# Additions of the diagonal behind all selects of their step, sums multiplied later, next block's rows loaded a phase sooner

## The chip, the cores and the metric

The kernel runs on one core of a Trainium2 chip. The metric is the device time of one execution in microseconds. Five engines matter: PE (TensorE, the matrix products), ACT (ScalarE, exponentials and copies), DVE (VectorE, row maxima and small vector work), POOL (GpSimd, masking and additions in SBUF) and SP (SyncE, which issues all transfers). Each engine runs its own instructions in program order and waits on semaphores for the others.

## What is computed

A pre-norm transformer layer in float32 on two sequences of 2048 rows and 512 columns: causal attention with 16 heads of 32 and rotary positions, then a linear layer to which two of eight low-rank experts are added per row.

```python
x = x + _L0_attn_ref(_layernorm(x), Wq, Wk, Wv, Wo)
x = x + _L0_ffn_ref(_layernorm(x), base_w, base_b, router_w, router_b, lora_A, lora_B)
# attention:
scores = jnp.einsum('bhqd,bhkd->bhqk', q, k) / math.sqrt(dk)
scores = jnp.where(causal[None, None], scores, -jnp.inf)
attn = jax.nn.softmax(scores, axis=-1)
ctx = jnp.einsum('bhqk,bhkd->bhqd', attn, v)
```

## The kernel before, in words

**Blocks and steps.** The 4096 rows are eight blocks of 512 (`BLK`), four per sequence; block `n` has place `j = n % 4` in its sequence. The 16 heads are four groups `g` of four. A step is one pair (block, group), written (n,g) here: 32 steps. In a step the keys up to the block's end are `NT*(j+1)` tiles of 128, of which the last four lie on the diagonal. A tile of the step with number `kt` is worked on for four heads at once.

**Two streams side by side.** `side_by_side` interleaves, on every engine, the row maxima of the next step (`row_maxima`, tiles `sm`, L384 to L405) with the weighing of the current one (`attend`). For each tile, `attend` multiplies keys with queries (`scores`, L523), subtracts the maxima with a second product (`shift`, L531), lets ACT take the exponentials into a tile `pt` (`weigh`, L546) and, on a diagonal tile, lets POOL zero what lies above the diagonal (the select, `affine_select`, L553). A tile of 512 columns is handled as two pairs of heads, so each diagonal tile has two selects. Tiles 1 and 3 of the diagonal share one buffer and one select, so that a step has three diagonal quads with six selects: the first tile, the pair, and the third tile.

**Phases.** Each `yield` of `side_by_side` ends a phase. Between phases the main loop hands out everything else: products due now (`between`), projections and the former block's output stages from the list `waiting` (paced by `credit`), entries of `aside` (loads, layer norms, parts of the division) and additions from `ready`. A tile whose `weigh` is over is multiplied with the values three phases later (`later(3, ...)`, `weighted`, L595, tile `av`). PE is in order, so a product that waits holds everything behind it.

**Sums of the weights.** The softmax denominators need the sum over all `pt` tiles. POOL adds tiles into the step's first tile, which has a buffer of its own kind (tag `acc`, two buffers): `add`, L616, one instruction per pair of heads. For the middle tiles of long steps (`SUMMED`) ACT sums beside the row maxima instead. So a step has adds for the diagonal tiles, and in blocks with j = 2 and 3 also for tiles 1 to 3. Each add is put on `ready` where its exponentials are issued. Every gap between phases drains `ready` from the front while the head's step is `weighed`, that is, while the step's first tile has been multiplied with the values. Before a tile takes one of the three `pt` buffers, `before` forces the adds and products of that buffer's former tile. After the last product of a step, ACT copies `av` away and `later(2, ...)` sets `summed`: it drains what is left of the step's adds and multiplies the sum tile with ones on PE (L623, tile `den`). The sums then go through DRAM to be spread over partitions (L649, L652), are inverted on DVE (`over_sums`, three phases later), come back broadcast (L658), and POOL multiplies the context by them (`over_all`, L665, three phases later again).

**Next block.** `start_block` sets four row loads (`xa`, L104, on SP, with the rotation tables behind the fourth), their layer norm (moments on DVE and POOL, scaling on ACT) and their transposition (`turned`, L159 on PE, L160 on ACT) at phases counted back from the block's begin by `EARLY` = 14; the first key projection (`kps`, L193) follows the last transposition. The row tiles share five buffers (tag `tmp`) with the rotation products, the normalised rows of the output stages and the tile `total` of the sums.

The cross-engine order on PE, ACT, DVE and POOL is the order in which these functions issue; the order on SP is chosen by the framework. The lines that the change touches: L560 (what is put on `ready`), `after` (L573), L611 (`later`), L766 to L769 (the phases of the next block) and L856 (the draining).

Of the kernel before, what the change touches and what calls it, by code (L numbers as in the profile page):

```python
# [23 lines left out]
NB = S // BLK  # L24
# [10 lines left out]
def preln_attention_moe_lora(  # L35
# [428 lines left out]
    ready = []  # L464

    def later(phases, tile, do):
        due.append((phase[0] + phases, tile, do))
        due.sort(key=lambda entry: entry[0])
# [19 lines left out]
    def attend(s):  # L488

        n, g, q, keys, values = s["n"], s["g"], s["q"], s["k"], s["v"]  # L490
        j = blocks[n][1]
        diagonal, beside = NT * j, SUMMED[j]

        summed_from = 0 if beside[0] else NT * beside[1]
        tiles = NT * (j + 1)
# [3 lines left out]
        pts, index = {}, {}  # L499
        s["av"] = None  # L500

        def low(kt):
            return max(kt - diagonal, 0) * P
# [7 lines left out]
        def quad(*kts):  # L511

            all_of = slice(0 if len(kts) > 1 else low(kts[0]), BLK)
            sc = {}

            def take(r):
                sc[r] = bank(f"sc_{n}_{g}_{kts[0]}_{r}")

            def scores(i, r):
                if i < len(kts):  # L520
                    jj, tt = divmod(kts[i], NT)
                    rows = slice(DK * r, DK * r + DK)
                    nc.tensor.matmul(  # L523
                        out=sc[r][:, place(kts[i])], lhsT=keys[jj][rows, bass.ts(tt, P)],
                        rhs=q[rows, low(kts[i]) :], start=True, stop=False,
                    )

            def shift(i, r):
                if i < len(kts):
                    rows = slice(DK * r, DK * r + 3)  # L530
                    nc.tensor.matmul(  # L531
                        out=sc[r][:, place(kts[i])], lhsT=ones_b[rows, :],
                        rhs=s["max"][rows, low(kts[i]) :], start=False, stop=True,
                    )

            def weigh(r):
                if kts[0] not in pts:
                    tag, bufs = ("acc", 2) if kts[0] == summed_from else ("pt", PTS)
                    pt = p2.tile(
                        [P, 4, BLK], F32, tag=tag, bufs=bufs, name=f"pt_{n}_{g}_{kts[0]}"  # L540
                    )
                    begun[0] += tag == "pt"
                    for kt in kts:
                        index[kt], pts[kt] = begun[0] if tag == "pt" else 1 << 30, pt
                pt = pts[kts[0]]
                nc.scalar.activation(pt[:, r, all_of], sc[r][:, all_of], AF.Exp)  # L546
                if kts[0] >= diagonal and r % 2:

                    at = all_of.start
                    on = pt[:, r - 1 : r + 1, at : at + len(kts) * P]  # L550
                    if len(kts) > 1:
                        on = on.rearrange("p h (k q) -> p h k q", q=P)
                    nc.gpsimd.affine_select(  # L553
                        out=on, in_=on, compare_op=ALU.is_ge, fill=0.0, base=0,
                        pattern=[[0, 2]] + [[0, len(kts)]] * (len(kts) > 1) + [[1, P]],
                        channel_multiplier=-1,
                    )
                if kts[0] != summed_from and not beside[0] <= kts[0] // NT < beside[1] and r % 2:
                    ready.extend(
                        (index[kts[0]], s, summed_from, lambda kt=kt: add(kt, r - 1)) for kt in kts  # L560
                    )

            def before():

                if kts[0] == summed_from:
                    return
                last = begun[0] + 1 - PTS
                while any(tile <= last for _, tile, _ in due):
                    due.pop(0)[2](2)
                while ready and ready[0][0] <= last:  # L570
                    ready.pop(0)[3]()

            def after():  # L573
                if len(kts) == 1:
                    lo = low(kts[0])
                    mid = (lo + BLK) // 2
                    halves = [(kts[0], lo, mid), (kts[0], mid, BLK)]
                else:
                    halves = [(kt, low(kt), BLK) for kt in kts]
                later(3, index[kts[0]], lambda many: weighted(halves, many))  # L580

            return before, take, scores, shift, weigh, after

        def weighted(halves, many):

            if s["av"] is None:
                s["av"] = ps_o.tile([P, BLK], F32, tag="av", name=f"av_{n}_{g}")
            whole = len(halves) == many == 2 and halves[0][0] == halves[1][0]
            now, left = halves[:many], halves[many:]
            for kt, lo, hi in [(halves[0][0], low(halves[0][0]), BLK)] if whole else now:  # L590
                jj, tt = divmod(kt, NT)
                at = place(kt).start - low(kt)
                for r in range(4):
                    rows = slice(DK * r, DK * r + DK)
                    nc.tensor.matmul(  # L595
                        out=s["av"][rows, lo:hi],
                        lhsT=values[jj][g][:, tt, rows],
                        rhs=pts[kt][:, r, at + lo : at + hi],
                        start=(kt == 0 and lo == 0),
                        stop=(kt == tiles - 2 and hi == BLK),  # L600
                    )
            if left:
                due.insert(0, (0, index[left[0][0]], lambda many: weighted(left, many)))
                return
            kt = halves[-1][0]
            if kt == summed_from:
                s["weighed"] = True
            if kt == tiles - 2:
                s["dest"] = wide.tile([P, BLK], F32, tag="ctx", bufs=6, name=f"ctx_{n}_{g}")
                nc.scalar.copy(s["dest"], s["av"])  # L610
                later(2, 1 << 31, summed)  # L611

        def add(kt, r):

            some = pts[summed_from][:, r : r + 2, low(kt) :]
            nc.gpsimd.tensor_add(some, some, pts[kt][:, r : r + 2, place(kt)])  # L616
# [134 lines left out]
    def set_aside(at, do):  # L751
        aside.append((at, do))
        aside.sort(key=lambda entry: entry[0])

    def wait(stage, at, not_before=0):
        waiting.append((at, len(waiting), not_before, stage))
        waiting.sort(key=lambda entry: entry[:2])

    def start_block(n):

        (load, measured, scaled, turned), heads, vals, made = prepare(n)
        keys[n], values[n], queries[n], contexts[n] = made["k"], made["v"], made["q"], []
        at = begin[NC * n]
        for t in range(NT):
            if n > 0:
                set_aside(at - EARLY + t, lambda t=t: load(t))  # L766
                set_aside(at - EARLY + 2 + t, lambda t=t: measured(t))
                set_aside(at - EARLY + 4 + t, lambda t=t: scaled(t))
                wait([(0.5, lambda t=t: turned(t))], at - 7 + t, at - 8 + t)  # L769
            else:  # L770
                load(t)
        if n == 0:
            for do in (measured, scaled, turned):
                for t in range(NT):
                    do(t)
        for g in range(NC):
            for i, stage in enumerate(heads[g]):
                if n == g == 0:
                    do_stage(stage)
                else:  # L780
                    here = begin[NC * n + g]

                    free = begin[NC * n + g - 1] + 3 if i else 0
                    wait(stage, here - 4 + i, max(free, at - 6))
            if g == 1:
                for stage in vals:
                    wait(stage, begin[NC * n + 1] + 1, at - 6)
# [9 lines left out]
    EARLY, BEHIND, AHEAD = 14, 3, 100  # L797
# [4 lines left out]
    for step in steps + [None]:  # L802
        maxima = []
        if step:
            n, g = step
# [4 lines left out]
            while len(queries[n]) <= g:  # L810
                do_stage(waiting.pop(0)[3])
            first = n - blocks[n][1]
            s = {
                "n": n, "g": g, "q": queries[n][g], "ctx": contexts[n],
                "k": [keys[m][g] for m in range(first, n + 1)],
                "v": [values[m] for m in range(first, n + 1)],
            }
# [3 lines left out]
        for i in range(slots):  # L821
# [3 lines left out]
            for _ in side_by_side(*todo):  # L825
# [27 lines left out]
                    given = given or us > 0.0  # L853
                if not given:
                    ahead()
                while ready and ready[0][1].get("weighed"):  # L856
                    ready.pop(0)[3]()
        late = part(weights, slots - 1, slots)
        if step:
            split()  # L860
            before, turned = s, turned_next
# [60 lines left out]
```

## Time and profile before

| | before |
|---|---|
| median of 3 runs | 2009.55 us (2005.08 to 2010.38) |
| the profiled execution's own time | 2002.71 us |
| its span, first to last instruction | 2000.9 us |
| mean granted TensorE clock | 0.966 |
| ACT busy | 1100.6 us |
| DVE busy | 1030.6 us |
| POOL busy | 936.8 us, of which L616 540.4 us and L553 92.7 us |
| DMA queues | 9.5% of 16 engines' span |
| chain that ended last | PE 77%, POOL 10%, ACT 6%, DVE 4% |

A group row of the profile reads: line, engine, operation, output<-inputs, shape, count | busy us, mean ns of one | idle us of that engine just before these instructions, and what ended most of it. "PEclk" in the slices is the clock that the throttle granted to TensorE, in tenths of full speed. POOL's groups on the critical lines:

```profile
L616 POOL TENSOR_TENSOR pt<-pt,pt 128x768 f32<-128x768 f32 (+2 forms) x320 | 540.4, 1702 | 65.2 <-PE av L595 35.2
L553 POOL TENSOR_SCALAR_AFFINE_SELECT pt<-pt 128x256 f32<-128x256 f32 (+1 forms) x192 | 92.7, 485 | 319.1 <-ACT pt L546 319.1
```

The chain by line, in the same execution, has 20% on L523, 11% on L595, 7% on L384 and 6% on POOL's L616.

### The profile page before, as it was taken

How to read it: one execution, taken by the hardware profiler on the slowest of the kernel's cores; microseconds unless marked ns; L12 is line 12 of the kernel's file. 1: busy time of each engine (PE TensorE's matmuls, PEld its weight loads, DVE VectorE, ACT ScalarE, POOL GpSimd, SP SyncE). 2: the span in 40 equal slices, each digit the busy share in tenths (PEclk: the TensorE clock that was granted, in tenths of full speed). 3: DMA queues.
4: the chain of work that ended last, by engine and by line, in shares of the span. 5: the costliest groups of instructions: out<-in, count | busy, mean ns of one | idle time of the engine just before them, and what ended most of it. 6: DMA issues, size and time to landing. Idle time of an engine off the chain costs nothing.

```text
span 2000.9 us, 34243 instructions
## 1 busy us (share of the span) xinstructions
PE 1869.0 (93%) x12880; PEld 760.7 (38%) x12880; DVE 1030.6 (52%) x2856; ACT 1100.6 (55%) x2653; POOL 936.8 (47%) x906
## 2 busy tenths in 40 slices
PE   7889989999989999998989999999999999999988
PEld 3334433334333333333334434333433333433434
DVE  3545555456555556563155556456555555555503
ACT  1346653456546676684533546545647466656851
POOL 3563434257464536154476344236545645434462
PEclk9899989899999999998999999999999999998999
DMA  4000111001200000100000112100011000020001
GB/s 163 22 12 13 55 32 43 6 7 39 78 14 7 1 28 28 59 23 1 22 18 18 38 59 70 51 15 7 22 49 59 2 6 7 22 65 7 7 7 43
DMA packets 42271, 61.19 MB, mean 31 GB/s; under 512 B 13180, under 2 KB 13692, under 8 KB 42104
## 3 DMA queue, kind: packets, MB, share of 16 engines
q1 hardware_dynamic: 42104, 59.00, 9.5%
q8 instruction: 101, 1.65, 0.3%
q14 instruction: 66, 0.54, 0.1%
HBM read 50.08 MB, written 8.90 MB: 29 GB/s over the span
## 4 chain that ended last, share of the span: by engine, by line
PE 77%; POOL 10%; ACT 6%; DVE 4%; issue 3%; DMA 1%; SPq 0%; ACTq 0%; POOLq 0%; DVEq 0%
PE sc L523 20%; PE av L595 11%; PE sm L384 7%; POOL pt L616 6%; PE qps L193 6%; PE kps L193 6%; PE vps L218 6%; PE yps L332 6%; PE ops L249 6%; PE sc L531 3%; ACT sm L405 3%; ACT pt L546 2%; PE den L623 1%; POOL pt L553 1%; PE yps L339 1%
## 5 line engine op out<-in xcount | busy, mean ns | idle before, releaser
L546 ACT ACTIVATE pt<-sc 128x512 f32<-128x512 f32 (+1 forms) x1152 | 600.2, 584 | 654.3 <-PE sc L531 570.3
L384 PE MATMUL sm<-k,q 32*128 32x512 f32 (+3 forms) x2560 | 691.6, 587 | 10.9 <-DVE pm L426 5.5
L397 DVE TENSOR_REDUCE pm<-sm 128x1 f32<-128x512 f32 x768 | 491.4, 684 | 318.1 <-PE sm L384 280.3
L523 PE MATMUL sc<-q,k 32*128 32x512 f32 (+3 forms) x2560 | 628.6, 588 | 2.6 <-ACT pt L546 1.5
L616 POOL TENSOR_TENSOR pt<-pt,pt 128x768 f32<-128x768 f32 (+2 forms) x320 | 540.4, 1702 | 65.2 <-PE av L595 35.2
L595 PE MATMUL av<-pt,v 128*32 128x256 f32 (+3 forms) x3440 | 330.2, 462 | 79.7 <-POOL pt L553 72.0
L405 ACT ACTIVATE sm<-sm,pm 128x512 f32<-128x512 f32 x512 | 345.2, 687 | 18.6 <-DVE pm L397 18.0
L392 DVE CUSTOM_DVE_ANT_0 sm<-sm,mask 128x128 f32<-128x128 f32 (+3 forms) x512 | 244.9, 512 | 130.0 <-PE sm L384 84.2
L523 PEld LDWEIGHTS sc<-q,k 32*128 32x128 f32 x2560 | 195.6, 188 | 295.7 <-issue 168.1
L384 PEld LDWEIGHTS sm<-k,q 32*128 32x128 f32 x2560 | 250.1, 188 | 63.7 <-ACT pt L546 23.7
L553 POOL TENSOR_SCALAR_AFFINE_SELECT pt<-pt 128x256 f32<-128x256 f32 (+1 forms) x192 | 92.7, 485 | 319.1 <-ACT pt L546 319.1
L531 PE MATMUL sc<-max,ones_b 3*128 3x512 bf16 (+3 forms) x1280 | 221.8, 352 | 0.0
L595 PEld LDWEIGHTS av<-pt,v 128*32 128x32 f32 x3440 | 72.2, 110 | 333.4 <-issue 209.6
L208 POOL TENSOR_TENSOR sw_k<-sw_k,sin 128x512 f32<-128x512 f32 x32 | 40.7, 1272 | 225.5 <-DVE sw_k L206 188.2
L193 PE MATMUL kps<-xnt_a,wk 128*128 128x512 f32 x256 | 128.7, 650 | 11.7 <-ACT xnt_a L160 11.7
L193 PE MATMUL qps<-xnt_a,wq 128*128 128x512 f32 x256 | 123.3, 626 | 3.7 <-ACT wq L190 3.7
L249 PE MATMUL ops<-wo,ctx 128*128 128x512 f32 x256 | 119.6, 612 | 3.9 <-POOL ctx L665 2.7
L332 PE MATMUL yps<-base_w,xnt_f 128*128 128x512 f32 x256 | 118.5, 606 | 4.0 <-DVE pm L426 4.0
L208 POOL TENSOR_TENSOR sw_q<-sw_q,sin 128x512 f32<-128x512 f32 x32 | 40.8, 1275 | 173.5 <-DVE sw_q L206 173.5
L405 ACT ACTIVATION_READ_ACCUMULATOR sm<-sm,pm 128x1 f32 x512 | 119.0, 232 | 0.0
L218 PE MATMUL vps<-wv,xnt_a 128*128 128x512 f32 x256 | 117.5, 604 | 0.0
L531 PEld LDWEIGHTS <-ones_b 3*128 3x128 bf16 x1280 | 64.4, 95 | 70.3 <-issue 61.5
(96 smaller groups left out, 1386.2 us busy)
## 6 DMA issues: line engine op xcount, KB each, us to landing
xa<-in_x SPq DMA_DIRECT2D x32, 256.0 KB
xf<-in_x SPq DMA_DIRECT2D x32, 256.0 KB
wo<-in_wo_t SPq DMA_DIRECT2D x8, 1024.0 KB
base_w<-in_base_wt SPq DMA_DIRECT2D x8, 1024.0 KB
out<-xf SPq DMA_DIRECT2D x32, 256.0 KB
sum<-over SPq DMA_DIRECT2D x124, 64.0 KB
cos<-in_cos SPq DMA_DIRECT2D x8, 256.0 KB
sin<-in_sin SPq DMA_DIRECT2D x8, 256.0 KB
```

The costliest lines, as they stand in the source:

```text
L193: nc.tensor.matmul(out=pj, lhsT=w[:, c, bass.ts(g, P)], rhs=held["xn_t"][:, c, :], start=(c == 0), stop=(c == NC - 1),)
L249: nc.tensor.matmul(out=po, lhsT=ctx_t[c][:, bass.ts(t, P)], rhs=held["w"][:, c, :], start=(c == 0), stop=(c == NC - 1),)
L332: nc.tensor.matmul(out=po, lhsT=held["xn_t"][:, c, bass.ts(t, P)], rhs=held["w"][:, c, :], start=(c == 0), stop=False,)
L384: nc.tensor.matmul(out=sc[r][:, some[i]], lhsT=q[rows, bass.ts(ts[i], P)], rhs=keys[c][rows, : wide_of[i]], start=True, stop=True,)
L392: nc.vector.tensor_tensor_reduce(sc[r][:, here], sc[r][:, here], mask[:, BLK - w :], 1.0, 3.0 * MASKED, ALU.add, ALU.max, pm[:, t, r, j : ...
L397: nc.vector.tensor_reduce(pm[:, t, r, c : c + 1], sc[r], AX.X, ALU.max, negate=True)
L405: nc.scalar.activation(sc[r], sc[r], AF.Exp, bias=pm[at], accum_out=s["se"][at])
L523: nc.tensor.matmul(out=sc[r][:, place(kts[i])], lhsT=keys[jj][rows, bass.ts(tt, P)], rhs=q[rows, low(kts[i]) :], start=True, stop=False,)
L531: nc.tensor.matmul(out=sc[r][:, place(kts[i])], lhsT=ones_b[rows, :], rhs=s["max"][rows, low(kts[i]) :], start=False, stop=True,)
L546: nc.scalar.activation(pt[:, r, all_of], sc[r][:, all_of], AF.Exp)
L595: nc.tensor.matmul(out=s["av"][rows, lo:hi], lhsT=values[jj][g][:, tt, rows], rhs=pts[kt][:, r, at + lo : at + hi], start=(kt == 0 and lo ...
L616: nc.gpsimd.tensor_add(some, some, pts[kt][:, r : r + 2, place(kt)])
```

## The change

An add on `ready` now says whether its tile lies ahead of the diagonal. Such an add may run, as before, once the step is `weighed`; an add of a diagonal tile only once the step is `over`, which is set when the step's last quad (with number `tiles - 2`) has been issued whole, its selects included. A gap issues at most one add (`if` for `while`). `summed` comes five phases after the last product instead of two in blocks with j > 0, except in the last two groups of each sequence's last block. The next block's loads, moments, scaling and transpositions all move one phase forward.

```diff
-                        (index[kts[0]], s, summed_from, lambda kt=kt: add(kt, r - 1)) for kt in kts
+                        (index[kts[0]], s, kts[0] < diagonal, lambda kt=kt: add(kt, r - 1)) for kt in kts
@@
             def after():
+                if kts[0] == tiles - 2:
+                    s["over"] = True
@@
-                later(2, 1 << 31, summed)
+                later(5 if j and not (j == NB - 1 and g >= 2) else 2, 1 << 31, summed)
@@
-                set_aside(at - EARLY + t, lambda t=t: load(t))
-                set_aside(at - EARLY + 2 + t, lambda t=t: measured(t))
-                set_aside(at - EARLY + 4 + t, lambda t=t: scaled(t))
-                wait([(0.5, lambda t=t: turned(t))], at - 7 + t, at - 8 + t)
+                set_aside(at - EARLY - 1 + t, lambda t=t: load(t))
+                set_aside(at - EARLY + 1 + t, lambda t=t: measured(t))
+                set_aside(at - EARLY + 3 + t, lambda t=t: scaled(t))
+                wait([(0.5, lambda t=t: turned(t))], at - 8 + t, at - 9 + t)
@@
-                while ready and ready[0][1].get("weighed"):
+
+                if ready and ready[0][1].get("weighed" if ready[0][2] else "over"):
                     ready.pop(0)[3]()
```

`add`, `before`, `weighted` and the number and shapes of all adds and selects are as they were.

## The prediction, made before the changed kernel ran

> **What bounds the kernel now.** I read the page's busy shares first, then its clock row, then who waits for whom, then one wait in the timeline.
>
> ```profile
> PE 1869.0 (93%) x12880; PEld 760.7 (38%) x12880; DVE 1030.6 (52%) x2856; ACT 1100.6 (55%) x2653; POOL 936.8 (47%) x906
> ...
>
> ...
> L595 PE MATMUL av<-pt,v 128*32 128x256 f32 (+3 forms) x3440 | 330.2, 462 | 79.7 <-POOL pt L553 72.0
> ```
>
> PE is the bound: no other engine passes 55%. It loses time in two ways. It idles 2000.9 - 1869.0 = 132 us, and it runs at a mean clock of 0.966, so up to 0.034 x 2000.9 = 68 us more. The last row says that 72.0 us of the idling come ahead of the product of a weight tile with the values, which waits for a select. The waits:
>
> ```profile
> PE av L595 <- POOL pt L553: 72.0, 28, 5.0
> ...
> PE kps L193 <- ACT xnt_a L160: 11.7, 8, 1.9
> ```
>
> 28 waits, up to 5.0 us. Why a select of 0.4 to 0.65 us is late, POOL's timeline around the longest shows, and PE's line beside it:
>
> ```profile
> 928.40 1.27 POOL L209 TENSOR_TENSOR k<-k,sw_k 128x512 f32<-128x512 f32 x1
> 929.62 2.36 POOL L616 TENSOR_TENSOR pt<-pt,pt 128x1024 f32<-128x1024 f32 x1
> 931.92 0.65 POOL L553 TENSOR_SCALAR_AFFINE_SELECT pt<-pt 128x512 f32<-128x512 f32 x1
> 932.65 2.60 POOL L616 TENSOR_TENSOR pt<-pt,pt 128x768 f32<-128x768 f32 x2
> 935.20 0.64 POOL L553 TENSOR_SCALAR_AFFINE_SELECT pt<-pt 128x512 f32<-128x512 f32 x1
> ```
> ```profile
> 935.89 1.51 PE L595 MATMUL av<-pt,v 128*32 128x384 f32 x8 [5.02 <-POOL pt L553]
> ```
>
> The second select of the pair could have run at about 930.5, when its exponentials end; two adds of 2.36 and 2.60 us sit in front of it. What follows such a wait is in the windows (PE busy, then the other engines, then the clock as the third number from the end):
>
> ```profile
> 388.50:402.20 13.70, 13.70 (x64) 4.97 (x57) 4.86 (x12) 6.36 (x15) 4.06 (x6) 0.50 0.00 1
> 402.30:416.00 13.70, 13.70 (x108) 4.70 (x106) 6.38 (x11) 7.51 (x17) 11.39 (x6) 1.00 0.02 3
> 920.00:930.80 10.80, 10.80 (x95) 4.97 (x94) 7.00 (x23) 3.26 (x6) 8.88 (x7) 1.00 0.01 2
> 934.60:948.20 13.60, 12.31 (x72) 3.45 (x72) 0.40 (x2) 6.42 (x14) 6.96 (x8) 0.50 0.01 1
> ```
>
> After the waits at 386.7 and 935.9 PE runs at half clock for 13.7 us.
>
> **Part 1, selects ahead of adds.** No instruction is added or removed: 320 adds (540.4 us) and 192 selects (92.7 us) stay. Of the 28 waits two belong to the last step (2.85 + 4.43 = 7.3 us at 1939.8 and 1945.9) and are treated under the end; 26 remain, 64.7 us. In the changed program's order on POOL the six selects of a long step follow each other with no add of that step between them, and in the short j = 0 steps at most one add of the step before stands ahead of a select, where before up to four stood in one block (5.18 us at 124.2). What remains: the pair's second select is still behind a key's rotation (1.27 + 1.26 us) in steps (1,2), (2,2), (5,2), (6,2). At 325.8 and 1305.6 this leaves 1.09 us today with no add in front, so I keep 4 x 1.1; about 0.35 us (ACT's end plus one select) for six other pairs, and 1 us at 1038.7: 7.5 us. **Saved: 64.7 - 7.5 = 57 us.** Bounds 40 and 65.
>
> **Part 2, the clock.** I went through the half-clock stretches that begin within a few us of those 26 waits: 95 us in 16 stretches; less the idling inside them, half is lost, 43 us. That is 0.66 us per us of wait. The Trainium skill ("TensorE: Matmul & The Clock Gate", sections on the clock gate and on its oscillation) says that PE goes to half clock after an idle window of about 3.4 us and advises against gaps beyond that. By the rule only the eight waits over 3.4 us would count, with one window of 3.4 us each: 8 x 1.7 = 14 us. But the row at 388.5 follows a wait of 1.92 us with 13.7 us of half clock, and waits of 2.8 us at 764.1 and 1739.3 are followed too. I take the trace: **57 x 0.66 = 38 us saved**; by the rule 14; ends 10 and 43.
>
> **Part 3, where the adds go.** In long steps all eight diagonal adds now come after the last select, by the rows:
>
> ```profile
> L616 POOL TENSOR_TENSOR pt<-pt,pt 128x1024 f32<-128x1024 f32 x128 | 298.3, 2355 | 53.8 <-PE av L595 35.2 <-ACT pt L546 16.8
> ...
> L616 POOL TENSOR_TENSOR pt<-pt,pt 128x768 f32<-128x768 f32 x64 | 115.7, 1807 | 2.8
> ```
>
> 2 x 2.36 + 2 x (1.81 + 0.73) + 2 x 1.27 = 12.3 us of POOL. They now stand in front of two things. First the next step's `pt` buffers: tile 1 needs the first two adds (4.7 us), tile 2 six (9.8 us), tile 3 all. PE takes two phases of 2.3 us or more per tile, so tiles 1, 2, 3 start about 5, 9 and 14 us after the last select: covered, barely. Where no maxima run beside, a tile takes about 3 us and POOL is late by 1 to 3 us; ACT has slack and PSUM a few banks, so little reaches PE. ACT waited for adds 8.6 us in all before. I take +4 us; ends 0 and 40.
>
> Second the sums. For j > 0 they come three phases later and the order leaves other POOL work or products between the last add and `den`. For j = 0 and step (3,3) it is still two phases while adds run one a gap: in (0,0), (0,1), (0,2), (3,3), (4,0), (4,1), (4,2) the last add stands behind a select of the next step, which waits for exponentials of scores issued just ahead of `den`. So `den` waits for two exponentials (0.66 us), a select (0.41), an add (1.27): about 2.4 us, 7 times = **17 us, and at 0.66 another 11 us of clock**. Before, `den` waited for adds 2.2 us in all, mostly weight loads. Behind `den` is all of PE. Ends 5 and 45.
>
> **Part 4, the end.** In the last step (7,3) POOL is busy from 1934.5 to 1948.6 with 2.0 us of selects and 12.3 us of adds, and `den` needs all. With the selects first, the adds start when the last exponential (1937.4) and its select are over, about 1937.8, and end at 1950.1: **+1.5 us**. The two waits on selects (7.3 us) turn into one of about 10 us ahead of `den`.
>
> **Part 5, sums later.** The division ends three phases later for j = 1, 2 and the first half of j = 3. The context is read by the output stages, which start later and are spread over fewer phases; `total` occupies one of the `tmp` buffers at another time. The longest POOL idling ahead of L665 was 14.3 us and no PE wait followed. 0; ends -2 and +8.
>
> **Part 6, rows a phase sooner.** SP issues 28 row loads and 7 pairs of tables sooner. For step (1,0) three loads now pass the broadcasts of the sums on SP, and wait there for transposes; the broadcasts' reader stands well behind those on POOL. DVE waited 3.0 us in all for rows, so nothing is gained there. The key projection waits 11.7 us for the last transposed rows; in the new PE order six score products, shifts and four value products stand between them only for blocks 3 and 7. There 1.90 us go, and the half clock that stretches the eight products from 3.70 to 5.40 us: 2 x 3.6 = **7 us saved**. Ends 0 and 12.
>
> **Sum.** -57 - 38 + 4 + 17 + 11 + 1.5 - 7 = -68.5 us. The profiled execution took 2002.7 us, so 1934; the median of the runs is 2009.55, 7 us above it, so 1941. I say **1940 us**.
>
> **Rivals.**
> (a) *The clock stays.* Half clock might follow PE's load as such and not the waits. Then -57 + 4 + 17 + 1.5 - 4 = -38: 1971 us. For it: the waits at 464.9 (1.45 us) and 1038.7 (3.12 us) are followed by no half clock. Against it: nearly every half-clock stretch lies at a wait.
> (b) *Slower: buffers come free too late.* If POOL's 12.3 us of adds aren't covered, ACT's exponentials of the next step's tiles 1 to 3 wait for adds, the scores' PSUM banks fill, and PE stops. It happened once before, at 1909.2: ACT waits 3.99 us and PE 1.27. There are 16 steps with j = 2 or 3; at 4.7 us each (one tile's two adds) with the clock's 0.66 this is 16 x 7.8 = 125 us instead of 4, so 2009.55 - 68.5 + 121 = 2062. It decides from about 4.4 us a step, where it eats the gain. Against it: POOL is at 47%, and the next step's first tile uses the other kind of buffer.
> (c) *It doesn't do what it says*: `before` forces adds ahead of selects, and the waits stay. The POOL order speaks against it. 2009 us.
> (d) *Sums hidden*: `den`'s waits don't show, 28 us less: 1913.
>
> **Numbers.** Forecast 0.62 (1918 to 1962), (a) 0.18, (b) 0.08, (c) 0.03, (d) 0.09. The range 1905 to 1985 leaves out (b), (c) and tails of (a) and (d), about 0.17. A measurement of this kernel tells about 0.3% (6 us) from no change: faster 0.89 (forecast, (a), (d)), same 0.03, slower 0.08.
>
> **What would show it.** PE's wait of L595 on selects falls from 72.0 to under 12 us; the clock rises to about 0.98; a wait of `den` on adds of 20 to 30 us appears, ten of them at the end; ACT's wait on adds stays under 25 us; `kps` still waits 8 us. Wrong if ACT's waits on adds pass 60 us, or if half-clock stretches stay as many as now.

## The result, and the profile after

| | before | changed |
|---|---|---|
| median of the runs, taken beside each other | 2009.97 us (2005.08 to 2016.66) | 2061.82 us (2060.63 to 2063.59) |
| ratio, 95% interval | | 1.0256 (1.0225 to 1.0287): slower |
| span of the profiled execution | 2000.9 us | 2061.0 us |
| mean granted TensorE clock | 0.966 | 0.948 |

The forecast was 1940 us; the time is 2062. First the page of the changed kernel, in the same rows as before (L595 has become L597, L616 L618, L623 L625):

```profile
PE 1924.9 (93%) x12904; PEld 783.9 (38%) x12904; DVE 1040.0 (50%) x2856; ACT 1102.3 (53%) x2653; POOL 935.5 (45%) x906
...
L384 PE MATMUL sm<-k,q 32*128 32x512 f32 (+3 forms) x2560 | 720.5, 592 | 28.9 <-ACT pt L546 14.9
...
L618 POOL TENSOR_TENSOR pt<-pt,pt 128x768 f32<-128x768 f32 (+2 forms) x320 | 537.2, 1699 | 20.5 <-ACT pt L546 10.0
...
L597 PE MATMUL av<-pt,v 128*32 128x256 f32 (+3 forms) x3464 | 332.5, 463 | 16.2 <-POOL pt L553 8.6
```

POOL does the same work in the same time (935.5 us, 936.8 before). The value products wait for selects 8.6 us instead of 72.0. Yet PE is busy 55.9 us longer at the same products, and it still idles 2061.0 - 1924.9 = 136 us. Who waits for whom says what came in place of the selects (us in total, times, longest):

```profile
ACT pt L546 <- POOL pt L618: 112.2, 45, 6.8
...
PE den L625 <- POOL pt L618: 46.9, 11, 10.3
...
PE sm L384 <- ACT pt L546: 14.9, 13, 3.3
...
PE sc L523 <- ACT pt L546: 13.2, 9, 2.5
...
PE av L597 <- POOL pt L553: 8.6, 14, 1.1
...
PE kps L193 <- ACT xnt_a L160: 7.1, 6, 2.9
```

The same rows before:

```profile
ACT pt L546 <- POOL pt L616: 8.6, 3, 4.0
...
PE sc L523 <- ACT pt L546: 1.5, 2, 1.3
...
PE sm L384 <- ACT pt L546: 0.2, 1, 0.2
PE den L623 <- POOL pt L616: 0.2, 1, 0.2
```

ACT's exponentials now wait for additions, PE waits for exponentials (14.9 + 13.2 = 28.1 us), and `den` waits for additions.

**Where `den` waits.** POOL's timeline in step (0,1) of the changed kernel (start, duration, what), then PE's:

```profile
83.02 1.81 POOL L618 TENSOR_TENSOR pt<-pt,pt 128x768 f32<-128x768 f32 x1
...
86.50 0.72 POOL L618 TENSOR_TENSOR pt<-pt,pt 128x256 f32<-128x256 f32 x1
...
95.28 1.27 POOL L208 TENSOR_TENSOR sw_q<-sw_q,sin 128x512 f32<-128x512 f32 x1 [7.61 <-DVE sw_q L206]
96.63 1.27 POOL L209 TENSOR_TENSOR q<-q,sw_q 128x512 f32<-128x512 f32 x1
97.85 1.83 POOL L618 TENSOR_TENSOR pt<-pt,pt 128x768 f32<-128x768 f32 x1
99.62 0.65 POOL L553 TENSOR_SCALAR_AFFINE_SELECT pt<-pt 128x512 f32<-128x512 f32 x1
100.23 0.73 POOL L618 TENSOR_TENSOR pt<-pt,pt 128x256 f32<-128x256 f32 x1
100.91 0.64 POOL L553 TENSOR_SCALAR_AFFINE_SELECT pt<-pt 128x512 f32<-128x512 f32 x1
101.51 1.27 POOL L618 TENSOR_TENSOR pt<-pt,pt 128x512 f32<-128x512 f32 x1
102.72 0.42 POOL L553 TENSOR_SCALAR_AFFINE_SELECT pt<-pt 128x256 f32<-128x256 f32 x1
103.10 1.27 POOL L618 TENSOR_TENSOR pt<-pt,pt 128x512 f32<-128x512 f32 x1
```
```profile
104.43 1.94 PE L625 MATMUL den<-pt,ones 128*32 128x512 f32 x8 [3.69 <-POOL pt L618]
106.30 1.12 PE L159 MATMUL xnps_a<-ident,xa 128*128 128x128 f32 x4
108.09 6.61 PE L193 MATMUL kps<-xnt_a,wk 128*128 128x512 f32 x8 [0.68 <-ACT xnt_a L160]
```

The six L618 rows are the additions of step (0,0). Two have gone by 87; then POOL idles 7.61 us in front of a query's rotation that waits for DVE, with four additions left, because these belong to later gaps and so stand behind the rotation in POOL's order. From 95.3 to 104.4 POOL works without a pause: the rotation, and the four additions one by one with the selects of step (0,1) between them. `den` of (0,0) needs the last addition. PE waits 3.69 us, and the eight `kps` products behind it take 6.61 us.

**Where the buffers come late.** POOL behind the last select of step (2,0), in the changed kernel:

```profile
473.92 2.36 POOL L618 TENSOR_TENSOR pt<-pt,pt 128x1024 f32<-128x1024 f32 x1
479.31 0.23 POOL L147 TENSOR_SCALAR mom_f<-mom_f 128x1 f32<-128x1 f32 x1 [3.03 <-DVE mom_f L146]
...
481.76 4.12 POOL L618 TENSOR_TENSOR pt<-pt,pt 128x1024 f32<-128x1024 f32 x2
...
488.57 3.31 POOL L618 TENSOR_TENSOR pt<-pt,pt 128x256 f32<-128x256 f32 x3
493.77 1.28 POOL L266 TENSOR_TENSOR xf<-xf,bias_sb 128x512 f32<-128x512 f32 x1 [1.89 <-ACT xn_f L153]
495.00 7.13 POOL L618 TENSOR_TENSOR pt<-pt,pt 128x512 f32<-128x512 f32 x4
```

The diagonal's additions are the first eight of these: one, two, three, and two of the last four. They begin at 473.9 and the eighth ends at about 497.5, when `den` starts: 23.6 us for 12.3 us of work, because work for the former block (moments of its layer norm, L147, and the bias, L266) stands between them and waits for DVE and ACT. ACT's timeline answers line by line:

```profile
484.13 1.09 ACT L546 ACTIVATE pt<-sc 128x512 f32<-128x512 f32 x2 [3.72 <-POOL pt L618]
...
487.60 1.12 ACT L546 ACTIVATE pt<-sc 128x512 f32<-128x512 f32 x2
...
491.91 1.09 ACT L546 ACTIVATE pt<-sc 128x512 f32<-128x512 f32 x2 [1.86 <-POOL pt L618]
...
494.28 1.08 ACT L546 ACTIVATE pt<-sc 128x512 f32<-128x512 f32 x2
497.52 1.09 ACT L546 ACTIVATE pt<-sc 128x512 f32<-128x512 f32 x2 [2.16 <-POOL pt L618]
```

Tiles 1, 2 and 3 of step (2,1) start exactly when the second, sixth and eighth addition are over (484.1, 491.9, 497.5). A fourth wait, at 510.9, holds PE 1.94 us; the window behind it (PE busy, and the clock as the third number from the end) has a clock of 0.59:

```profile
511.54 1.61 PE L523 MATMUL sc<-q,k 32*128 32x512 f32 x4 [1.94 <-ACT pt L546]
```
```profile
511.50:521.80 10.30, 10.26 (x31) 3.35 (x32) 2.92 (x7) 6.15 (x16) 5.19 (x3) 0.59 0.17 57
```

I cut both traces at each step's product for the transposed maxima (L435) and compared step by step. "Short" is the eight stretches (0,1), (0,2), (0,3), (1,0) and (4,0) to (4,3), in which the sums of the j = 0 steps (but for (4,3)) and of (3,3) fall; "other" is the rest between (1,1) and (7,2):

| us of the profiled span | before | changed |
|---|---|---|
| short | 246.7 | 292.4 |
| other | 1570.6 | 1576.7 |
| start, (0,0) and (7,3) | 183.6 | 191.9 |

Against before, +45.7, +6.1 and +8.3 us. That the other steps come out even could be a gain cancelled by a loss, or no gain at all. The experiments tell which.

### The profile page after: what moved, and what is told of

Read it like the earlier page. It is cut to its first block, busy times and chain, and to the rows that moved or that the text cites. A ratio compares the mean times of both kernels' runs of the same rounds, so it can differ in the third digit from the quotient of the medians.

```text
span 2061.0 us, 34292 instructions
## 1 busy us (share of the span) xinstructions
PE 1924.9 (93%) x12904; PEld 783.9 (38%) x12904; DVE 1040.0 (50%) x2856; ACT 1102.3 (53%) x2653; POOL 935.5 (45%) x906
## 4 chain that ended last, share of the span: by engine, by line
PE 78%; POOL 10%; DVE 5%; ACT 4%; issue 3%; DMA 0%; ACTq 0%; POOLq 0%; DVEq 0%
PE sc L523 20%; PE av L597 12%; PE sm L384 9%; POOL pt L618 6%; PE kps L193 6%; PE qps L193 6%; PE yps L332 6%; PE vps L218 5%; PE ops L249 5%; PE sc L531 3%; ACT pt L546 2%; PE den L625 2%; DVE sm L392 1%; PE yps L339 1%; PE den L631 1%
## 5 line engine op out<-in xcount | busy, mean ns | idle before, releaser
L384 PE MATMUL sm<-k,q 32*128 32x512 f32 (+3 forms) x2560 | 720.5, 592 | 28.9 <-ACT pt L546 14.9
L523 PE MATMUL sc<-q,k 32*128 32x512 f32 (+3 forms) x2560 | 635.9, 586 | 14.2 <-ACT pt L546 13.2
L618 POOL TENSOR_TENSOR pt<-pt,pt 128x768 f32<-128x768 f32 (+2 forms) x320 | 537.2, 1699 | 20.5 <-ACT pt L546 10.0
L597 PE MATMUL av<-pt,v 128*32 128x256 f32 (+3 forms) x3464 | 332.5, 463 | 16.2 <-POOL pt L553 8.6
L384 PEld LDWEIGHTS sm<-k,q 32*128 32x128 f32 x2560 | 260.4, 188 | 98.5 <-ACT pt L546 50.5
L597 PEld LDWEIGHTS av<-pt,v 128*32 128x32 f32 x3464 | 73.2, 110 | 274.6 <-issue 220.6
```

Of the source, the lines that this page charges most:

```text
L384: nc.tensor.matmul(out=sc[r][:, some[i]], lhsT=q[rows, bass.ts(ts[i], P)], rhs=keys[c][rows, : wide_of[i]], start=True, stop=True,)
L523: nc.tensor.matmul(out=sc[r][:, place(kts[i])], lhsT=keys[jj][rows, bass.ts(tt, P)], rhs=q[rows, low(kts[i]) :], start=True, stop=False,)
L597: nc.tensor.matmul(out=s["av"][rows, lo:hi], lhsT=values[jj][g][:, tt, rows], rhs=pts[kt][:, r, at + lo : at + hi], start=(kt == 0 and lo ...
```

## The experiments

**Theory A**: what costs is how the additions are handled (held until the last select, one a gap). **Theory B**: the later sums or the sooner rows cost by themselves. In each table the ratio is to runs of the kernel before on the same chip.

### Each part alone

`e1_adds_only` has the edits to the additions only, `e2_sums_only` the `later` line only, `e3_rows_only` the four phases of the next block only; each is the kernel before with those lines of the change's diff.

> The kernel before with the new rule for additions alone (held back until the step's last select, one a gap); sums still multiplied two phases after the last product, rows loaded as before. Theory A (holding the additions back is what costs: they release the pt buffers late and end late for the sums): slower than before by as much as the whole change or more, since den is now multiplied two phases after the last product in every step: 2060 to 2110 us; ACT's wait of its exponentials (L546) on additions (L618) about 100 us, den's wait on additions over 60 us. Theory B (later sums and sooner rows are what costs): the gain I forecast comes out, 1940 to 1985 us, with ACT's wait on additions under 40 us.

> The kernel before with the later sums alone. Theory A (the held additions cost): 2000 to 2016 us, within 0.3% of before, with den's wait on additions and ACT's wait on additions as before (0.2 and 9 us). Theory B (later sums and sooner rows cost): 2030 to 2060 us.

> The kernel before with the next block's rows a phase sooner, alone. Theory A: 2000 to 2012 us; PE's wait of kps (L193) on ACT falls from 11.7 to about 7 us and nothing else moves. Theory B (later sums and sooner rows cost): 2025 us or more, with longer waits of ACT, DVE or PE for tmp buffers or rows.

| | median, us | ratio (95%) | PE `den` on additions, us | ACT on additions, us |
|---|---|---|---|---|
| e1_adds_only | 2104.86 | 1.0444 (1.0412 to 1.0476) | 116.7 | 88.4 |
| e2_sums_only | 2014.86 | 0.9988 (0.9961 to 1.0015) | | |
| e3_rows_only | 2018.59 | 1.0029 (1.0005 to 1.0053) | | |

Theory B falls: the sums alone change nothing, the rows alone cost at most 0.5%. The additions alone cost more than the whole change; the later sums give part of it back, since in e1 `den` comes two phases after the last product in every step. In e3 `kps` waits 9.9 us instead of 11.7 (I expected 7), and its time is above the 2000 to 2012 us that I expected; the kernel before takes 2014.56 us on that chip.

### Without the limit of one a gap

```diff
-                if ready and ready[0][1].get("weighed" if ready[0][2] else "over"):
+                while ready and ready[0][1].get("weighed" if ready[0][2] else "over"):
```

> The changed kernel, but a gap drains all additions that may run instead of one at most. Theory A1 (the den waits of the short steps come from additions going one a gap, and are the larger part, some 46 us with the half clock after them): den's wait on additions falls from 46.9 to under 25 us and the time to 2015 to 2045 us. Theory A2 (what costs is that the additions wait for the last select at all, so pt buffers come free late): the eight additions still start after the last select and end at most a few us sooner, so ACT's wait on additions stays over 80 us and the time stays at 2050 to 2075 us.

It took 1950.57 us, ratio 0.9663 (0.9626 to 0.9701). Neither expectation held: `den`'s wait fell, as A1 has it, but ACT's fell too, which A2 thought would stay. One word decides between 2.6% slower and 3.4% faster. POOL's timeline at the same places as above, behind the last select of (0,0) and of (2,0), with `den` of (0,0) between them:

```profile
83.34 7.64 POOL L618 TENSOR_TENSOR pt<-pt,pt 128x768 f32<-128x768 f32 x6
```
```profile
101.00 1.06 PE L625 MATMUL den<-pt,ones 128*32 128x512 f32 x8
```
```profile
441.26 12.30 POOL L618 TENSOR_TENSOR pt<-pt,pt 128x1024 f32<-128x1024 f32 x8
```

The six additions of (0,0) now end at 91.0, ahead of the rotation, and `den` does not wait for them. The eight of (2,0) take 12.30 us in a row. The waits of this kernel:

```profile
ACT pt L546 <- POOL pt L618: 16.6, 10, 4.7
...
PE av L597 <- POOL pt L553: 11.7, 16, 2.6
...
PE den L625 <- POOL pt L618: 10.3, 1, 10.3
```

What is left of `den`'s wait is the one at the end. PE's busy time is back at 1869.6 us.

### The limit without holding back

The kernel before, with `if` in place of `while` in its own draining line.

> The kernel before with one edit: a gap issues at most one addition; additions may still run once the step's first tile is weighed, sums two phases after the last product, rows as before. Theory C (the limit of one addition a gap is the cost by itself: the additions are spread over as many gaps in POOL's order as there are additions and stand behind whatever POOL does there): 2050 to 2110 us, den's wait on additions over 60 us, though L595's wait on selects falls from 72.0 to under 50 us. Theory D (the limit costs only because the additions are also held back until the last select): 1990 to 2020 us, den's wait under 20 us.

It took 2014.48 us, ratio 1.0027 (1.0006 to 1.0048). Theory C falls for the time. But D's reason is only half right, as the waits of this kernel show:

```profile
PE den L623 <- POOL pt L616: 39.5, 11, 5.7
...
PE av L595 <- POOL pt L553: 30.9, 21, 4.2
```

By itself the limit takes 72.0 - 30.9 = 41 us off the selects and puts 39 us on `den`: it moves a wait rather than being free. (ACT's wait on additions rises too, from 8.6 to 31.4 us.)

### Splitting the loss

`e6_short_while` is the changed kernel with the limit lifted where the next addition belongs to a j = 0 step:

```diff
-                if ready and ready[0][1].get("weighed" if ready[0][2] else "over"):
+                while ready and ready[0][1].get("weighed" if ready[0][2] else "over"):
                     ready.pop(0)[3]()
+                    if not ready or blocks[ready[0][1]["n"]][1]:
+                        break
```

> The changed kernel, but without the limit of one addition a gap where the additions belong to a block with j = 0; in all other blocks one a gap as changed. Theory C (the cost has two separate parts: den waits of the short steps, some 41 us in the table of steps, and late pt buffers in the long ones, some 65 us): 2015 to 2030 us, den's wait on additions 16 to 20 us, ACT's wait on additions still about 100 us. Rival (the short steps carry it all): 1950 to 1970 us.

`e9_forced_sooner` keeps the limit everywhere but has `before` force additions for a buffer one tile sooner:

```diff
-                while ready and ready[0][0] <= last:
+                while ready and ready[0][0] <= last + 1:
```

> The changed kernel, one a gap kept, but what must be added before a tile takes its pt buffer is forced one tile sooner. Theory E (in the long steps the loss is that additions, one a gap, stand behind POOL's other work and waits, so that a buffer is released only when the next tile already wants it): ACT's wait of exponentials on additions falls from 112 to under 50 us, PE's waits on exponentials from 28 to under 10 us, and the time to 1960 to 2010 us. Rival F (POOL's 12.3 us of additions in a row are what ACT waits for, wherever they stand): ACT's wait stays over 90 us and the time at 2050 us or more.

`e10_two_a_gap` runs the changed `if` twice in each gap:

```diff
-                if ready and ready[0][1].get("weighed" if ready[0][2] else "over"):
-                    ready.pop(0)[3]()
+                for _ in range(2):
+                    if ready and ready[0][1].get("weighed" if ready[0][2] else "over"):
+                        ready.pop(0)[3]()
```

> The changed kernel with a limit of two additions a gap. If the loss follows the number of gaps over which eight additions are spread (Theory E), most of it goes: 1955 to 1985 us, den's wait on additions 10 to 20 us, ACT's wait on additions 20 to 50 us. If any limit costs: 2010 us or more.

Spans and stretches are of the profiled execution. e4 ran on another chip than e6, e9 and e10, so ratios, not medians, are to be compared.

| | median, us | ratio (95%) | span | short | other |
|---|---|---|---|---|---|
| changed | 2061.82 | 1.0256 (1.0225 to 1.0287) | 2061.0 | 292.4 | 1576.7 |
| e6_short_while | 2009.91 | 1.0002 (0.9978 to 1.0026) | 2008.2 | 248.8 | 1569.6 |
| e9_forced_sooner | 1979.50 | 0.9841 (0.9814 to 0.9868) | 1978.8 | 275.8 | 1510.3 |
| e4_while | 1950.57 | 0.9663 (0.9626 to 0.9701) | 1949.6 | 245.3 | 1511.7 |
| e10_two_a_gap | 1943.47 | 0.9664 (0.9638 to 0.9691) | 1944.6 | 236.4 | 1515.8 |

The two parts are separate. e6 takes the short steps close to where e4 has them and leaves the others (its time is 5 us below what I expected); e9 does the others and only part of the short ones. Their waits, first e6's:

```profile
ACT pt L546 <- POOL pt L618: 105.3, 40, 6.8
...
PE den L625 <- POOL pt L618: 16.3, 4, 10.3
```

Then e9's:

```profile
PE den L625 <- POOL pt L618: 33.5, 8, 6.1
...
PE av L597 <- POOL pt L553: 19.8, 20, 3.9
...
ACT pt L546 <- POOL pt L618: 8.5, 7, 2.8
```

So the long steps lose 1576.7 - 1511.7 = 65 us because buffers come free late: with the limit of one a gap still there, but what a buffer needs forced a tile sooner, ACT's wait goes from 112.2 to 8.5 us and the time with it. In these stretches PE idles 53 us in the changed kernel and 32 in e4, and is busy 1523.8 us and 1480.0: two thirds of the 65 us show as slower products, not as idling. An estimate, half of the half-clock time that falls into PE's busy time, puts 28 of those 44 us down to the clock (54 us in the changed kernel, 26 in e4); the other 16 stay open. Theory E holds and F falls. (e9 also puts some additions ahead of the step's own last selects; the selects' wait of 19.8 us is the price.) Two a gap are enough: 27.4 us of ACT's wait on additions and 11.7 us of `den`'s remain, and the ratio is that of e4 without any limit; the time is below my 1955 to 1985.

### What the rest is worth without the limit

`e7_while_adds_only` is e1 with the `while`; `e11_while_no_rows` adds the later sums; e4 adds the sooner rows. `e8_while_end_old` is e4, and `e12_end_old_no_rows` is e11, each with the old rule in the last step:

```diff
-                        (index[kts[0]], s, kts[0] < diagonal, lambda kt=kt: add(kt, r - 1)) for kt in kts
+                        (index[kts[0]], s, kts[0] < diagonal or (n, g) == steps[-1], lambda kt=kt: add(kt, r - 1)) for kt in kts
```

> The kernel before with the additions held back until the last select, but without the limit of one a gap; sums two phases after the last product and rows as before. If the selects ahead of additions bring the whole gain: 1945 to 1960 us, like the changed kernel without the limit (1950.6). If the later sums are needed to hide the 12.3 us of additions that follow the last select: 1965 to 2000 us, with den waiting for additions 1 to 3 us in each of the 16 to 20 longer steps.

> The changed kernel without the limit of one addition a gap, and in the very last step (7,3) the additions may run once the step's first tile is weighed, as before. By the table of steps the last step took 106.3 us before and 112.2 us in the changed kernel without the limit: 5 us less than 1950.6, so 1941 to 1949 us, with den's last wait of 10.3 us gone and two waits on selects of 3 to 5 us back. If the end is set by POOL's work as such and not by its order: 1950 us.

> The changed kernel without the limit and with the next block's rows loaded as before; it splits the 21 us between e7_while_adds_only (1972.0) and e4_while (1950.6). If they come from the later sums: 1948 to 1958 us, no den wait but the last. If from the rows: 1965 to 1972 us.

> As e11_while_no_rows, and in the last step (7,3) the additions may run once the step's first tile is weighed. By the table of steps 5 to 7 us less than e11_while_no_rows on the same chip; if rows sooner cost 3 us or so as alone (ratio 1.0029), 1938 to 1946 us, the fastest version.

| | additions | sums | rows | end | median, us | ratio (95%) |
|---|---|---|---|---|---|---|
| e7_while_adds_only | new, no limit | | | | 1972.00 | 0.9801 (0.9767 to 0.9835) |
| e11_while_no_rows | new, no limit | later | | | 1940.73 | 0.9638 (0.9604 to 0.9673) |
| e4_while | new, no limit | later | sooner | | 1950.57 | 0.9663 (0.9626 to 0.9701) |
| e12_end_old_no_rows | new, no limit | later | | old | 1938.19 | 0.9650 (0.9606 to 0.9695) |
| e8_while_end_old | new, no limit | later | sooner | old | 1943.56 | 0.9667 (0.9627 to 0.9707) |

The later sums bring 1.6% (31 us between the medians): in e7 `den` waits 23.4 us, nine times, of which 13.1 us in eight steps before the end (I expected 1 to 3 us in each of 16 to 20); in e11 once, 10.3 us, at the end. The sooner rows bring nothing that can be seen, and neither does the old rule at the end: the intervals of the last four rows lie over each other. In e8 the last wait of `den` is gone (0.2 us in all) and the selects' wait is 18.0 us instead of 11.7, as expected; the 5 us that I expected of it can't be told from none. These four, with e10, are the fastest versions, some 3.5% faster than before. I had expected e11 7 us or more slower than it is.

## Why the prediction was wrong

**What bounds the kernel, and part 1: right.** The selects' wait was to fall from 72.0 to under 12 us; it fell to 8.6 (11.7 in e4). What it brought in time is less than forecast; see the sum below.

**Part 3, the buffers: the step that failed.** It read "tile 1 needs the first two adds (4.7 us), tile 2 six (9.8 us), tile 3 all", against tiles that start "about 5, 9 and 14 us after the last select". The durations were right (12.30 us in a row in e4), but I put eight additions one behind the other when the change lets out one a gap, in program order behind POOL's other work. In the changed kernel the three releases come 10.2, 18.0 and 23.6 us after the first addition starts (484.1, 491.9, 497.5 less 473.9). I had called the tiles "covered, barely"; measured from the first addition they are late by 5 to 10 us, and since a late tile delays the next, ACT waits 3.7, 1.9 and 2.2 us. I took +4 us with an end at 40; the long steps lost 65. Of the signs that I named for being wrong, ACT's wait on additions (over 60 us) stood at 112.2, and the half-clock stretches grew from 28 to 35.

**Part 3, the sums: right place, wrong size.** I had 7 waits of `den` of 2.4 us and 11 us of clock, 28 us. The changed kernel has 11 waits: 10.3 us at the end, two of 1.1 us in (2,1) and (6,1), and eight in the short stretches, 34.3 us in all or 4.3 each. These stretches lose 292.4 - 245.3 = 47 us against e4. I had counted one last addition behind one select that waits for its exponentials. In the trace from 83.0 four additions are left when POOL idles for DVE, and the last three each stand behind a select of the new step, so the delays add up. The eighth stretch that I had not counted is (1,0), with the sums of (0,3).

**Part 2, the clock: near in size, but not set by these waits alone.** I priced a us of wait removed at 0.66 us of clock, 38 us, and set aside the rule of the Trainium skill ("TensorE: Matmul & The Clock Gate", the sections on the clock gate and on its oscillation), by which only idle gaps over about 3.4 us count and which gave an estimate of 14 us. Count as the clock's loss one minus its mean, times the span, in the median of a version's runs, and compare with runs of the kernel before on the same chip. This loss falls by 27 us in e4 and e8 (83.5 to 56.5, 76.3 to 49.5) and by 40 us in e11 and e12 (78.3 to 38.8 and 37.8), all well above 14. PE's waits on selects and of `den` together fall by 50 us in e4 and 49 in e11, so a us of them went with 0.54 us of clock in one and 0.8 in the other. What differs between e4 and e11, and between e8 and e12, is only the rows' phase: these waits alone don't set the clock. Single runs scatter, from 0.971 to 0.980 in e4 and from 0.969 to 0.983 in e12. In the changed kernel the clock did not rise to about 0.98, as forecast, but fell: its loss is 0.052 x 2061.0 = 107 us in the profiled execution, against 68 in that of the kernel before.

**Part 4, the end: small.** +1.5 us foreseen; the last step takes 111.9 us instead of 106.3, with the one wait of 10.3 us as described.

**Part 5, the later sums: 0, right only alone.** By themselves 0.9988. With the additions behind the selects they are worth 31 us without the limit and, with the sooner rows, 1.9% or some 38 us with it (ratios 1.0444 and 1.0256): they are the cover that lets 12 us of additions follow the last select. I counted that cover as given.

**Part 6, the rows: no gain.** `kps` waits 4.6 us less in the changed kernel, 1.8 with the rows alone, but no time follows; alone the ratio is 1.0029. The clock's loss, counted as above, is some 13 us larger with the rows sooner than without in all three pairs: e3 and the kernel before (96.8 and 83.5), e4 and e11, e8 and e12. Why is open. The 7 us were not there.

**The sum.** I was off by 120 us: -68.5 forecast, +51.5 measured (by the ratio). The limit costs 119 us (ratios 1.0256 and 0.9663), where I had 4 + 28 = 32: 87 us too few. The other 33 are gains that did not come: parts 1, 2, 4 and 6 make 57 + 38 - 1.5 + 7 = 100.5 us, and e4, which has them all without the limit, gains 68. The selects' wait fell as forecast and the clock's gain came 11 us short; where the rest went, no run here shows.

**The rivals.** The mechanism of (b), buffers free too late, banks filling, PE stopping, is what happened in the long steps. Its 2062 us agrees with the result by chance: it had 125 us there and no more on `den` than the forecast; the runs have 65 us there and 47 in the short steps. That e11 takes the forecast's 1940 us is chance too: it has no wait of `den` but the last, 28 us less than foreseen, and smaller gains. What was wrong is thus in the main one edit, `if` for `while`, described in the change: in the term of the buffers I gave it nothing, in that of the sums one addition. I argued that the adds follow the last select, and not how many gaps they need.

## What to carry to other kernels

On an in-order engine a limit of "so many a gap" spreads work over the program order, not over time: price it by what stands between the pieces and what that waits for, not by the sum of the pieces' durations. Work that is taken off one critical wait has to end before the next deadline, here a buffer's release and a sum, so list each deadline with the last piece it needs and the gap in which that piece is issued. And when an edit bundles an order with a rate limit, test the two apart: here the order, with the later sums, was worth 3.6% (e11), the limit by itself cost 0.3% (e5), and the limit on top of the order and the rest cost 6% (1.0256 / 0.9663).

## What was not expected of the hardware

A busy PE is not the same work: at the same products its busy time was 1924.9 us in the changed kernel, 1868.0 in e9 and 1850.9 in e11. Most of this is the granted clock, which is 1 or 0.5 in every record of these traces. By an estimate, half of the half-clock time that falls into PE's busy time, it costs 91, 57 and 34 us; without it 1834, 1811 and 1817 us are left. For the 17 to 23 us between these there is only a guess: where ACT is late for a bank, the score and maxima products, which else overlap in the timeline, may run with less beside them (L384 is busy 720.5 us in the changed kernel and 686.6 in e11, the clock's part included).

Again waits of PE were followed by half clock: 1.94 us at 509.6 by a window of 10.3 us at 0.59, and 3.69 us at 100.7 by `kps` products of 6.61 us, which take 3.70 us in e4. Nearly all half-clock stretches in these traces (341 of 354) last 3.4 us or two to five times as long. No run here isolates what makes one of them longer than another.
